# LSTM stage of a 12-sublayer decoder: the inputs' product on four column groups of 32 tokens, one copy of the turned input ahead of it, and the context loaded behind the weights

## The chip, the cores and the metric

One core of a Trainium2 chip. The metric is the device time of one execution in microseconds (us); lower is better. The kernel is one launch; its weights are repacked on the host beforehand.

## The reference, cut to what matters

The reference runs twelve sublayers on x of 8 sequences x 112 tokens x 256 features, in float32. Only the first is touched: an attention whose queries and keys come out of two LSTMs.

```python
def _lstm(x, Wih, Whh, b):
    xW = jnp.einsum('bsd,gd->sbg', x, Wih) + b          # the inputs' product
    h0 = jnp.zeros((x.shape[0], Whh.shape[1]), x.dtype)
    def step(carry, xt):
        h, c = carry
        gates = xt + h @ Whh.T                          # the recurrent product
        i, f, g, o = jnp.split(gates, 4, axis=-1)
        c = jax.nn.sigmoid(f) * c + jax.nn.sigmoid(i) * jnp.tanh(g)
        h = jax.nn.sigmoid(o) * jnp.tanh(c)
        return ((h, c), h)
    _, hs = jax.lax.scan(step, (h0, h0), xW)
...
x = x + _L0_attn_ref(_layernorm(x, axis=-1), L0_attn_Wih_q, L0_attn_Whh_q, L0_attn_b_q, ...)
```

Each LSTM has 256 hidden features (1024 gates) and 112 steps, which follow one another. A later sublayer, L0_xattn, is the first that reads the context `ctx_512` (8 x 375 x 128).

## The kernel before, in words

**Loads.** The constructor issues, on SyncE's DMA queue (SP), x, the constants (the identity among them) and a small vector, and then the first eight weight blobs into a ring of eight buffers (`_Ring.load`, L358); a further blob is issued when one has been used up, the next of them only when the LSTMs are over. The context, turned (`ctxT`, 1.5 MB), is issued on ScalarE's queue at L393, at the same time as x. The first two blobs are the q LSTM's input and recurrent weights, the next two those of the k LSTM, the fifth the biases.

**Ahead of the LSTMs (`ln_T_mm`).** The layer norm (L464 to L474, VectorE) writes `xn`. TensorE turns it in four quarters: two halves of four sequences by two halves of the features (L546, four transposes of 112x128 into a PSUM tile `mm`, of which there are two). Each quarter is copied out of PSUM twice: by VectorE into `xs`, in the order [feature half, block of 16 tokens, sequence, token] (L552), and by ScalarE into `xnT`, in the order of tokens (L556). `xs` is the stationary operand of the inputs' product; `xnT` that of the values.

**The inputs' product (`product`, L585).** One block of 16 tokens of all 8 sequences is 128 columns. `inputs(m, l, a, n)` multiplies block m with n gate columns of LSTM l, in two matmuls over the feature halves; two adds on VectorE (L610) take the result out of PSUM, add the bias and write `xw`. Block 0 of both LSTMs is computed ahead of the loop, in products of 512 columns; everything else comes from the generator `pieces`, one matmul at a time: blocks 1 to 6 in products of 256 columns, and then the values of the eight sequences (112 tokens by 256). Two pieces are taken ahead of the loop and 110 in its steps, so steps 110 and 111 have none.

**The loop (`lstm`).** Its order is written out by hand for TensorE, VectorE and ScalarE. In each step t, for LSTM l = 0 and then 1:
- L652: the recurrent product onto the gates `g`, eight matmuls, two for each of four column groups. The state `hT` is 32 columns wide, and group j writes partitions 32j to 32j+31 with a quarter of the gates.
- L615: `from_inputs` begins the gates of step t+1, four matmuls, one for each column group, which pick the step's rows out of `xw`.
- for l = 1, one piece of the inputs' product, L585 (here 128 columns wide).
- L665 and L666 (ScalarE): sigmoid and tanh of the gates; L671, L673, L674 (VectorE): the cell; for l = 1 an add of the inputs' product, L610; L678 (ScalarE): tanh of the cell; L680, L682 (VectorE): h, and its turned form `hT`, which L652 of the next step reads.
- L683 (GpSimd): a copy of `hT` into `hs`, which the attention reads after the loop.

A float32 matmul stands in the profile as two loads (PEld) and two matmuls (PE).

`cp` copies out of PSUM by VectorE and ScalarE in turn, from one flag for the whole kernel.

Of the kernel before, what the change touches and what calls it, by code (L numbers as in the profile page):

```python
# [31 lines left out]
P = 128  # L32
S, NB, D = 112, 8, 256
T = S * NB
HT = T // 2
HB = NB // 2
# [299 lines left out]
def drain(steps):  # L336

    while True:
        try:
            next(steps)  # L340
        except StopIteration as stop:
            return stop.value


class _Ring:


    def __init__(self, nc, pool, src, where, used):
        self.nc, self.pool, self.src, self.where, self.used = nc, pool, src, where, used
        self.tiles, self.dead = [], 0  # L350
        self.load()
# [22 lines left out]
class _Kernel:  # L374
    def __init__(self, ctx, tc, args, plan):
        self.tc, self.nc, self.args = tc, tc.nc, args
        nc = self.nc
        where, used, self.vw, self.cw = plan
        pool = ctx.enter_context(tc.tile_pool(name="keep", bufs=1))
        self.small = ctx.enter_context(tc.tile_pool(name="small", bufs=4))  # L380
        ring = ctx.enter_context(tc.tile_pool(name="ring", bufs=NBUF))
        self.n = 0
        self.turn = 0
        self.x = pool.tile([P, NB, D], F32, tag="x", name="x")
        nc.sync.dma_start(self.x[:S], args["in_x"].rearrange("b s d -> s b d"))
        nv, ncst = args["in_vec"].shape[1], args["in_const"].shape[1]
        self.cst = pool.tile([P, ncst], F32, tag="cst", name="cst")
        nc.sync.dma_start(self.cst, args["in_const"])
        self.vec = pool.tile([P, nv], F32, tag="vec", name="vec")
        nc.sync.dma_start(self.vec, args["in_vec"])  # L390
        self.w = _Ring(nc, ring, args["in_w"], where, used)
        self.ctxT = pool.tile([P, NB * CTX], F32, tag="ctxT", name="ctxT")
        nc.scalar.dma_start(self.ctxT, args["in_ctxT"])  # L393
        self.xn = pool.tile([P, NB, D], F32, tag="xn", name="xn")
        self.xnT = pool.tile([P, 2, T], F32, tag="xnT", name="xnT")
        self.ident = self.c("ident")
# [141 lines left out]

    def ln_T_mm(self, ps, xs):

        drain(self.normalise(self.x, self.xn))
        for half in range(2):
            for kc in range(2):
                tp = self.t(ps, [P, 512], "mm")
                for j in range(HB):
                    self.nc.tensor.transpose(  # L546
                        tp[:, j * S : (j + 1) * S],
                        self.xn[:S, half * HB + j, kc * P : (kc + 1) * P],
                        self.ident[:S, :S],
                    )  # L550
                bs = slice(half * HB, (half + 1) * HB)
                self.nc.vector.tensor_copy(  # L552
                    xs[:, kc, :, bs, :].rearrange("p m b r -> p b m r"),
                    tp[:, :HT].rearrange("p (b m r) -> p b m r", b=HB, r=16),
                )
                self.nc.scalar.copy(self.xnT[:, kc, half * HT : (half + 1) * HT], tp[:, :HT])  # L556

    def lstm(self, hs, xs, vv, ps0):

# [7 lines left out]
        nc, tc, w = self.nc, self.tc, self.w  # L569
# [5 lines left out]
        with tc.tile_pool(name="ps_lstm", bufs=2, space=PSUM) as ps, tc.tile_pool(  # L575
# [5 lines left out]

            def product(pm, lhsT, rhs, outs):

                for k in range(2):
                    nc.tensor.matmul(pm, lhsT[k], rhs[:, k, :], start=k == 0, stop=k == 1)  # L585
                    if k == 1:
                        adds.extend((out, pm[:, part], row) for out, part, row in outs)
                    yield

            def inputs(m, l, a, n):  # L590
                pm = self.t(ps0, [P, 512], "mm")[:, :n]
                steps = [xs[:, k, m, :, :].rearrange("p b r -> p (b r)") for k in range(2)]
                outs = []
                for at in range(0, n, n // 2):
                    cols = slice(a + at, a + at + n // 2)
                    outs.append((xw[:, l, m, cols], slice(at, at + n // 2), bias[l][:, cols]))
                return product(pm, steps, wih[l][:, :, a : a + n], outs)

            def values(b):
                pm = self.t(ps0, [P, 512], "mm")[:S, :D]  # L600
                out, outs = vv[:S, b].rearrange("p h d -> p (h d)"), []
                for cols in (slice(0, P), slice(P, D)):
                    outs.append((out[:, cols], cols, bv[:S, cols]))
                return product(pm, self.tokens(b), wv, outs)
# [40 lines left out]
            with tc.manual_schedule(engines={ET.PE, ET.DVE, ET.Activation}):  # L645
                for t in range(S):
                    for l in range(2):
                        g = gs[l]
                        if t > 0:
                            for c in range(2):  # L650
                                for j in G:
# [4 lines left out]
                                        start=False,  # L656
                                        stop=c == 1,
                                        skip_group_check=True,
# [1861 lines left out]
```

## Time and profile before

| | us |
|---|---|
| median of 3 runs | 2295.76 (2290.16 to 2302.23) |
| the profiled execution | 2297.48, its span 2295.6 |
| TensorE busy | 2095.2 (91%) |
| VectorE busy | 1353.8 (59%) |
| ScalarE busy | 813.3 (35%) |
| first LSTM step begins (first sigmoid, L665) | 33.48 |
| last recurrent product (L652) begins | 408.58 |

"Span" is the time from the first to the last instruction of the profiled execution. A busy TensorE is one that has matmuls in flight; their ends are modelled, so starts are the safer thing to read. In the timeline the columns are the start in us, the length of the group in us, the engine, the line and operation, output<-inputs, the array's rows*columns and the shape, the number of records, and in brackets how long the engine was idle before and what ended that. In the waits they are: who waited, for whom, the total in us, how often, and the longest.

### The profile page before, as it was taken

What the parts mean: (1) busy time and instruction counts of PE and PEld (TensorE: products, weight loads), DVE (VectorE), ACT (ScalarE), POOL (GpSimd) and SP (SyncE); (2) the same over time, 40 slices, a digit from 0 to 9 for tenths busy, and PEclk for the clock granted to TensorE, in tenths of its full rate; (3) what the DMA queues carried; (4) which work ended last, traced back from release to release, by engine and by line L of the source; (5) the groups of instructions that cost most, each with busy time, mean ns of one, the idle gap of its engine ahead of it and who ended that gap; (6) DMA issues with size and microseconds to landing.
All of it is one profiled execution on the core that took longest, in us unless ns stands there. A gap on an engine that the chain in (4) does not pass through costs nothing.

```text
span 2295.6 us, 43649 instructions
## 1 busy us (share of the span) xinstructions
PE 2095.2 (91%) x17192; PEld 1261.1 (55%) x17192; DVE 1353.8 (59%) x3894; ACT 813.3 (35%) x2336; POOL 207.5 (9%) x406
## 2 busy tenths in 40 slices
PE   6999999898998999899898988999999999799944
PEld 3444444465666566546575555566655556556623
DVE  4666666586355677643666665676710314767788
ACT  2444444461112456420232224665221011256522
POOL 0111111002012000000003422000000000100000
PEclk9999999898999999999999999999999998999956
DMA  5000001002000000011001011001200100000000
GB/s 196 3 2 2 2 21 36 31 20 101 0 1 15 19 2 20 19 34 49 1 19 38 20 64 37 2 2 38 74 37 29 44 0 1 1 1 2 2 0 16
DMA packets 9889, 57.49 MB, mean 25 GB/s; under 512 B 1114, under 2 KB 2906, under 8 KB 4698
## 3 DMA queue, kind: packets, MB, share of 16 engines
q1 hardware_dynamic: 9108, 50.01, 6.0%
q8 instruction: 137, 2.24, 0.4%
q0 software_dynamic: 432, 3.15, 0.4%
q10 hardware_dynamic: 144, 1.54, 0.2%
q14 instruction: 68, 0.56, 0.1%
HBM read 53.77 MB, written 0.92 MB: 24 GB/s over the span
## 4 chain that ended last, share of the span: by engine, by line
PE 81%; DVE 13%; ACT 3%; issue 2%; POOL 1%; DMA 0%; DVEq 0%; POOLq 0%; ACTq 0%
PE mm L428 31%; PE g L652 9%; PE gu L428 7%; PE tr L1247 6%; PE g L615 4%; PE sc L428 4%; PE mm L585 3%; PE tr L428 3%; PE av L1263 3%; PE s L428 1%; PE mm L804 1%; DVE xn L474 1%; DVE xnm L1234 1%; PE s L751 1%; PE av L428 1%
## 5 line engine op out<-in xcount | busy, mean ns | idle before, releaser
L652 PE MATMUL g<-w,hT 128*32 128x256 f32 x3552 | 236.3, 383 | 1.1 <-DVE hT L682 0.8
L1234 DVE TENSOR_REDUCE xnm<-sc 112x1 f32<-112x375 f32 x384 | 184.5, 540 | 40.8 <-PE sc L428 40.2
L1247 PEld LDWEIGHTS tr<-cst,xe 112*125 112x125 f32 x1152 | 151.4, 188 | 94.8 <-issue 37.7
L1247 PE MATMUL tr<-cst,xe 112*125 112x112 f32 x1152 | 193.0, 289 | 6.8 <-DVE xeT L1255 4.2
L428 PE MATMUL mm<-hT,w 128*128 128x448 f32 x512 | 193.0, 539 | 0.0
L652 PEld LDWEIGHTS g<-w,hT 128*32 128x32 f32 x3552 | 94.7, 109 | 107.7 <-DVE hT L682 33.1
L428 PEld LDWEIGHTS mm<-hT,w 128*128 128x128 f32 x512 | 97.1, 190 | 94.4 <-issue 94.4
L428 PE MATMUL mm<-xnT,w 128*128 128x448 f32 x316 | 134.8, 568 | 8.0 <-DVE qT L1216 2.9
L1253 ACT COPY xeT<-tr 125x336 f32<-125x336 f32 x192 | 85.4, 445 | 158.4 <-PE tr L1247 158.1
L615 PE MATMUL g<-xw,cst 128*32 128x256 f32 x1792 | 137.8, 379 | 0.0
L1255 DVE COPY xeT<-tr 125x336 f32<-125x336 f32 x192 | 97.2, 506 | 68.7 <-PE tr L1247 61.8
L428 PE MATMUL mm<-w,hT 128*112 128x256 f32 x576 | 131.2, 387 | 0.3 <-DVE x L2042 0.3
L1238 ACT ACTIVATE xe<-sc,xnm 112x375 f32<-112x375 f32 x256 | 126.6, 583 | 7.3 <-DVE xnm L1234 7.3
L428 PE MATMUL gu<-xnT,w 128*128 128x448 f32 x320 | 124.3, 543 | 1.6 <-DVE hT L1401 1.2
L428 PEld LDWEIGHTS mm<-w,hT 128*112 128x112 f32 x576 | 102.9, 181 | 26.5 <-issue 2.9
L678 ACT ACTIVATE th<-cell 128x64 f32<-128x64 f32 x224 | 57.4, 256 | 158.8 <-DVE cell L674 158.1
L2365 DVE COPY wq<-tr 128x256 bf16<-128x256 bf16 (+1 forms) x12 | 4.6, 420 | 162.7 <-PE tr L2364 162.7
L665 ACT ACTIVATE sg<-g 128x192 f32<-128x192 f32 x224 | 74.1, 331 | 73.4 <-PE g L652 63.1
L428 PEld LDWEIGHTS mm<-xnT,w 128*128 128x128 f32 x316 | 59.4, 198 | 65.7 <-issue 42.5
L428 PE MATMUL mm<-w,oT 128*112 128x256 f32 x304 | 80.3, 410 | 16.3 <-DVE oT L1875 5.3
L428 PEld LDWEIGHTS gu<-xnT,w 128*128 128x128 f32 x320 | 59.3, 190 | 61.0 <-issue 54.0
L428 PE MATMUL sc<-xkT,qT 32*112 32x375 f32 x768 | 89.8, 519 | 0.0
(451 smaller groups left out, 3647.2 us busy)
## 6 DMA issues: line engine op xcount, KB each, us to landing
w<-in_w SPq DMA_DIRECT2D x33, 1024.0 KB, 4.9
raw<-in_wq POOLq DMA_DIRECT2D x3, 1024.0 KB, 5.3
cx<-in_ctx SPq DMA_DIRECT2D x2, 1500.0 KB
w<-in_w SPq DMA_DIRECT2D x3, 896.0 KB, 4.7
wi<-in_wint SPq DMA_DIRECT2D x3, 768.0 KB, 6.0
w<-in_w SPq DMA_DIRECT2D x2, 768.0 KB, 4.1
ctxT<-in_ctxT ACTq DMA_DIRECT2D x1, 1500.0 KB, 7.9
w<-in_w SPq DMA_DIRECT2D x2, 512.0 KB, 3.5
```

Source lines behind the costliest of these rows:

```text
L428: self.nc.tensor.matmul(out, lhsT, rhs, start=i == 0, stop=i == len(pairs) - 1)
L585: nc.tensor.matmul(pm, lhsT[k], rhs[:, k, :], start=k == 0, stop=k == 1)
L615: nc.tensor.matmul(g[32 * j : 32 * j + 32, :], pick[:, t % 16, :], xw[:, l, t // 16, 256 * j : 256 * j + 256], start=True, stop=t == 0, sk ...
L652: nc.tensor.matmul(g[32 * j : 32 * j + 32, :], hT[l][:, c, :], whh[l][:, c, 256 * j : 256 * j + 256], start=False, stop=c == 1, skip_group ...
L665: nc.scalar.activation(sg[:, :192], g[:, :192], AF.Sigmoid)
L678: nc.scalar.activation(th, cell[l], AF.Tanh)
L1234: nc.vector.tensor_reduce(nm, sc, AX.X, ALU.max, negate=True)
L1238: nc.scalar.activation(e, sc, AF.Exp, bias=nm)
L1247: nc.tensor.transpose(tp[:CH, i * S : (i + 1) * S], e[:, i * CH : (i + 1) * CH], self.ident[:S, :S])
L1253: nc.scalar.copy(eT, src)
L1255: nc.vector.tensor_copy(eT, src)
L1263: nc.tensor.matmul(avs[b][32 * j : 32 * j + 32, c * S : (c + 1) * S], values[b % 2][:CH, i, 4 * c + j, :], eTs[b, c, j][:, i, :], start=i ...
```

## The change

- `product`: each matmul of 128 (or 112) columns is cut into four of 32 (for 112: three of 32 and one of 16), each writing its own 32 partitions of the PSUM tile.
- `ln_T_mm`: each turned quarter is copied out of PSUM once, into `xs`, by `cp`, so by VectorE and ScalarE in turn; GpSimd copies from `xs` to `xnT`.
- the constructor: `ctxT` is issued on SyncE's queue, behind the first eight weight blobs.

```diff
-        nc.scalar.dma_start(self.ctxT, args["in_ctxT"])
+        nc.sync.dma_start(self.ctxT, args["in_ctxT"])
...
         drain(self.normalise(self.x, self.xn))
         for half in range(2):
+            bs = slice(half * HB, (half + 1) * HB)
             for kc in range(2):
-                tp = self.t(ps, [P, 512], "mm")
-                for j in range(HB):
-                    self.nc.tensor.transpose(
-                        tp[:, j * S : (j + 1) * S],
-                        self.xn[:S, half * HB + j, kc * P : (kc + 1) * P],
-                        self.ident[:S, :S],
-                    )
-                bs = slice(half * HB, (half + 1) * HB)
-                self.nc.vector.tensor_copy(
-                    xs[:, kc, :, bs, :].rearrange("p m b r -> p b m r"),
-                    tp[:, :HT].rearrange("p (b m r) -> p b m r", b=HB, r=16),
-                )
-                self.nc.scalar.copy(self.xnT[:, kc, half * HT : (half + 1) * HT], tp[:, :HT])
+                o = xs[:, kc, :, bs, :].rearrange("p m b r -> p b m r")
+                self.cp(o, self.turned(self.xn, ps, kc, half, "mm").rearrange("p (b m r) -> p b m r", b=HB, r=16))
+                o2 = self.xnT[:, kc, half * HT : (half + 1) * HT]
+                nc.gpsimd.tensor_copy(o2.rearrange("p (b m r) -> p b m r", b=HB, r=16), o)
...
+                n = lhsT[0].shape[-1]
                 for k in range(2):
-                    nc.tensor.matmul(pm, lhsT[k], rhs[:, k, :], start=k == 0, stop=k == 1)
+                    for a in range(0, n, 32):
+                        r = slice(a, min(a + 32, n))
+                        nc.tensor.matmul(
+                            pm[r], lhsT[k][:, r], rhs[:, k, :], start=k == 0, stop=k == 1, skip_group_check=True
+                        )
```

`turned` is the helper that other stages use already: the same four transposes into a tile of the same two buffers.

More of the change, by code (lines that the diff above doesn't have):

```diff
@@ L539, in ln_T_mm @@
     def ln_T_mm(self, ps, xs):
+        nc = self.nc
         drain(self.normalise(self.x, self.xn))
         for half in range(2):
+            bs = slice(half * HB, (half + 1) * HB)
             for kc in range(2):
-                tp = self.t(ps, [P, 512], "mm")
-                for j in range(HB):
-                    self.nc.tensor.transpose(
-                        tp[:, j * S : (j + 1) * S],
-                        self.xn[:S, half * HB + j, kc * P : (kc + 1) * P],
-                        self.ident[:S, :S],
-                    )
-                bs = slice(half * HB, (half + 1) * HB)
-                self.nc.vector.tensor_copy(
-                    xs[:, kc, :, bs, :].rearrange("p m b r -> p b m r"),
-                    tp[:, :HT].rearrange("p (b m r) -> p b m r", b=HB, r=16),
-                )
-                self.nc.scalar.copy(self.xnT[:, kc, half * HT : (half + 1) * HT], tp[:, :HT])
+                o = xs[:, kc, :, bs, :].rearrange("p m b r -> p b m r")
+                self.cp(o, self.turned(self.xn, ps, kc, half, "mm").rearrange("p (b m r) -> p b m r", b=HB, r=16))
+                o2 = self.xnT[:, kc, half * HT : (half + 1) * HT]
+                nc.gpsimd.tensor_copy(o2.rearrange("p (b m r) -> p b m r", b=HB, r=16), o)
     def lstm(self, hs, xs, vv, ps0):
```

## Prediction

> **What bounds the kernel now.** I read the page's table of engines and its chain first. TensorE is busy for 91% of the span and carries 81% of the chain, so work taken off TensorE counts, if nothing else ends last in the same place. The change touches two places only: the first 33 us, and the LSTM loop from 35 to 410 us. For the loop I took the timeline of TensorE over one step in the middle and over the last two steps, then the waits of its weight loads between 34 and 408 us.
>
> ```profile
> 282.24 1.07 PE L652 MATMUL g<-w,hT 128*32 128x256 f32 x16
> 283.12 0.61 PE L615 MATMUL g<-xw,cst 128*32 128x256 f32 x8
> 283.56 1.07 PE L652 MATMUL g<-w,hT 128*32 128x256 f32 x16
> 284.45 0.61 PE L615 MATMUL g<-xw,cst 128*32 128x256 f32 x8
> 284.99 0.70 PE L585 MATMUL mm<-w,xs 128*128 128x256 f32 x2
> ...
> 403.93 1.07 PE L652 MATMUL g<-w,hT 128*32 128x256 f32 x16
> 404.81 0.61 PE L615 MATMUL g<-xw,cst 128*32 128x256 f32 x8
> 405.24 1.05 PE L652 MATMUL g<-w,hT 128*32 128x256 f32 x16
> 406.11 0.61 PE L615 MATMUL g<-xw,cst 128*32 128x256 f32 x8
> 407.12 1.07 PE L652 MATMUL g<-w,hT 128*32 128x256 f32 x16 [0.40 <-DVE hT L682]
> ```
>
> A step is: recurrent product of the first LSTM (L652), its gates from inputs (L615), the same for the second LSTM, then a piece of the inputs' product (L585). From start to start, the groups take 0.88, 0.44, 0.89, 0.54, and after L585 0.63 (the next L652 starts at 285.62): 3.38 us. Over the whole loop, L652 of step 1 starts at 35.28 and that of step 110 at 403.93: 368.65 over 109 steps, 3.38 as well. Step 110 is the one step with no L585 behind it: 407.12 less 403.93 is 3.19, and there TensorE sat idle for 0.40 and waited for hT.
>
> ```profile
> PEld mm L585 <- issue: 45.3, 110, 0.4
> PEld g L652 <- DVE hT L682: 32.3, 109, 0.9
> PEld g L652 <- DVE cell L671: 18.3, 55, 0.3
> ```
>
> Ahead of each L585 the weight loads stand still for 0.41 with no releaser ("issue"), although every other group's loads run ahead (L615's at 282.91, 0.21 before its matmuls). L585's load and matmul start together (284.99), and so do those of the L652 behind it (285.62). So going from 128x32 pieces to a 128x128 product and back empties the array both times. In the first row on L652 the second LSTM waits for its hT; the row that names cell is the first LSTM after L585, and its hT was ready at 285.37 (L682, 285.13 plus 0.24), 0.25 before: there the array was late, not hT.
>
> **The loop's product on column groups.** Two records (128 wide) become eight (32 wide), the shape of L615's x8, which frees the array after 0.44 (283.12 to 283.56) with four groups side by side. So L585 takes 0.44 where it took 0.63, and the L615 ahead of it 0.44 where it took 0.54: TensorE's own step is 0.88+0.44+0.89+0.44+0.44 = 3.09, 0.29 less. That is not the gain, because hT is late next. First LSTM: L652's start to its L682 is 2.89 (282.24 to 285.13), and from there to the next L652 0.30 (406.82 to 407.12): 3.19. Nothing in that chain changes, so no step is shorter than 3.19. Second LSTM: in the last steps it took 3.34 (405.24 to 408.58), because its L671 stands on VectorE behind the first LSTM's L682 and starts 0.57 after the start of its own sigmoid (406.42 to 406.99), against 0.37 for the first (405.12 to 405.49). That is a matter of offset: it started 1.31 behind the first and ended 1.46 behind. At 1.46 its sigmoid comes 0.15 later against the same L682, the queueing falls from 0.20 to 0.05, and its chain to 3.19. From offset 1.46 TensorE still has 0.89+0.44+0.44 to do, which is over at 3.23, against hT at 3.19; should the array be late, the offset shrinks, which frees it again. So I expect a step between 3.19 and 3.23, and take 3.21: 0.17 less over 109 steps, **18.5 us**. Bounds: 20.7 at 3.19; nothing at 3.38; a loss if the pieces do not run side by side (a rival). The eight products of the values (the last 16 pieces) have 112 tokens, so a fourth group of 16 columns: priced as one of 32. VectorE's add (L610) keeps its place, as does every instruction behind the LSTMs on each engine: four calls of the alternating copy leave its turn as it was.
>
> **A rule against this.** L615's loads at 282.91 start while L652's last matmuls stream until about 283.12, in the same rows of the array. The Trainium skill ("TensorE: Matmul & The Clock Gate", Part 3, The mechanism) says that weight loads overlap matmuls in flight only where the row group differs, and the column pieces all have the same row group. The trace disagrees; by the rule the eight loads would be exposed, which is the rival on the other side below.
>
> **Context behind the weights.** The start hangs on x:
>
> ```profile
> ctxT<-in_ctxT ACTq DMA_DIRECT2D x1, 1500.0 KB, 7.9
> x<-in_x SPq DMA_DIRECT2D x1, 896.0 KB, 10.1
> ...
> DVE st L464 <- DMA x<-in_x: 10.8, 1, 10.8
> ```
>
> Both are issued at 0.75 and share the engines, whose busy share is about 1.0 from 3 to 30 us. ctxT lands first, at 8.6; x at 10.84. Between 3 and 8.6 us some 400 GB/s moved, so 1.54 MB less ahead of x is worth **3.8 us**; x would land near 7. Bounds: 0, if x's small packets are its own limit; 5.3, if x lands like a 896 KB weight blob (4.7 after issue, 5.5). Every weight comes as much sooner: the bias of L610 (fifth blob) is 8.5 MB down the line now and 6.95 then, which the rates by window put at about 20.3, while L610 would want it near 21.3 (26.14 less 4.8). That margin of 1 us hides it. On SP's queue ctxT comes after the eight weight blobs (issued by 13.3); the next entry there is only issued at 408. ctxT's first reader is at 539.6. ScalarE loses an issue of 0.41 that nobody waited for.
>
> **One copy ahead.** Now each turned quarter is copied twice out of PSUM, by VectorE (0.62) and then ScalarE (0.53); the third quarter's transposes wait for ScalarE until 20.04, and L585 until 22.33. Then VectorE and ScalarE copy alternate quarters at once: the third transposes start at 19.45, TensorE is through the last quarter near 21.4, the first L585 follows there. **0.9 us**. A ScalarE copy with this stride isn't in the trace: 0.53 (its plain copy) to 0.62 (VectorE's same shape), which moves this by 0.1. The four copies that GpSimd gains are bounded by its 112x512 copy (0.62) and its 112x512 tensor_scalar (1.50): 2.5 to 6 us, from about 16, ahead of its hs copies, of which the first comes at about 30. The next reader of xnT is the values at 352.7. Hidden; if they were late, hs would queue and hT's writer with it, for a few steps.
>
> **The products before the loop** lose three changes of shape (27.75, 28.30, 32.79), at 0.10 to 0.19 each by the loop's rows: **0.4 us**. At the start the first L585 records take 0.85 instead of 0.43 for 3.6 us; I leave that as it is. The Trainium skill ("TensorE: Matmul & The Clock Gate", What's actually happening) has the clock released after one full window of about 3.4 us of activity, on a grid that doesn't start with the kernel; by it the half rate could last up to twice 3.4 us, and the sum would be up to 1.6 us smaller.
>
> **Sum.** 18.5+3.8+0.9+0.4 = 23.6. The profiled execution took 2297.48 (span 2295.6), 1.7 above the median 2295.76. So 2273.9 for that execution, and 2272 against the median. About 0.5% (11.5 us) is what a measurement can tell here: faster is below 2284.3.
>
> **Rivals.** (1) The recurrence keeps the step. If the second LSTM's 3.34 stays, as its last step shows, the loop gains 0.04 x 109 = 4.4, with the start 9.5: 2286, no change. For it: that row. Against it: the offset, which grows in that very step. 11%. (2) Slower: the loads of the column pieces are exposed, as the rule above has it. Eight loads of 0.109 are 0.87, the step 3.09+0.87 = 3.96, 0.58 more over 109 steps, 63; the 80 loads before the loop 8.7, less the start's 5.1: 67 slower, 2362. It decides from some 0.3 exposed per step. For it: L585's loads stand still now. Against it: the 48 loads of L615 and L652 in each step have the same shape and are covered wherever hT is there in time. 8%. (3) x lands no earlier: 3.8 less, 2276. Inside the forecast's range.
>
> **How the numbers follow.** Forecast with (3) 80%, a slip between it and (1) 1%. Low end: step at 3.19 and x at 5.5 give 3.7 more, and the runs shown reach 5.6 below their median: 2263. High end: rival (1) with a little spread, 2287. Outside is rival (2) and the tail of (1). Faster 0.80, same 0.12, slower 0.08.
>
> **What would show it.** Right: L652 of the first LSTM every 3.2 us; no "issue" idle ahead of L585's loads; L652 waiting for hT in both LSTMs, offset near 1.45; L585 x8 in 0.6; x landing near 7; first L585 before 18. Wrong: a step over 3.3, loads of L585 that start with their matmuls, L585 to next L652 over 0.5, or the clock at 0.5 inside the loop (1.00 in every window now), which would double TensorE's 3.09 of a step.

## The result, and the profile after

The changed kernel takes 2266.43 us, the median of 3 runs (2266.06 to 2273.7), against 2295.76. The ratio is 0.9885, 95% interval 0.986 to 0.9909: some 26 us, of which the interval allows 21 to 32. Its profiled execution took 2266.43, span 2264.7, so 30.9 less of span than the one of before. Predicted were 23.6.

The timeline of a middle step, with the same columns as before (L651 is the recurrent product, L614 the gates from inputs, L582 the inputs' product):

```profile
272.78 1.06 PE L651 MATMUL g<-w,hT 128*32 128x256 f32 x16
...
273.65 0.61 PE L614 MATMUL g<-xw,cst 128*32 128x256 f32 x8
...
274.22 1.07 PE L651 MATMUL g<-w,hT 128*32 128x256 f32 x16
...
275.11 0.61 PE L614 MATMUL g<-xw,cst 128*32 128x256 f32 x8
...
275.54 0.61 PE L582 MATMUL mm<-w,xs 128*32 128x256 f32 x8
...
275.99 1.07 PE L651 MATMUL g<-w,hT 128*32 128x256 f32 x16
```

From the first LSTM's recurrent product to its next one it is 3.21 us (272.78 to 275.99), where it was 3.38. The product has eight records and gives the array back after 0.45, where it took 0.63; L614 ahead of it takes 0.43, where that took 0.54. The second LSTM now starts 1.44 behind the first, where it started 1.32 behind.

The waits of the weight loads inside the loop had five rows before (34 to 408 us), with 45.3 us of "issue" at their head. Three stand in the prediction. The larger of the other two is the first LSTM again, right behind the product, put down to another instruction of VectorE that had just ended; the first row below is that one, of before. After (28 to 386 us) a single row is left, the second below:

```profile
PEld g L652 <- DVE tmp L673: 16.7, 50, 0.3
```

```profile
PEld g L651 <- DVE hT L681: 82.9, 218, 0.9
```

Nothing stands still ahead of the product any more, and of the 222 recurrent products in steps 1 to 111, of both LSTMs, 218 wait for hT. The bound has passed from the array to the recurrence. In the same stretch of steps the product's loads run while the matmuls of L614 stream:

```profile
271.91 0.61 PE L614 MATMUL g<-xw,cst 128*32 128x256 f32 x8
272.13 0.35 PEld L582 LDWEIGHTS mm<-w,xs 128*32 128x32 f32 x8
...
272.35 0.61 PE L582 MATMUL mm<-w,xs 128*32 128x256 f32 x8
```

The start, by the DMA issues and by the waits of the first 36 us:

```profile
x<-in_x SPq DMA_DIRECT2D x1, 896.0 KB, 5.8
```

```profile
DVE st L464 <- DMA x<-in_x: 6.5, 1, 6.5
DVE xw L609 <- DMA w<-in_w: 3.7, 1, 3.7
```

x lands 5.8 us after its issue instead of 10.1, and the layer norm begins at 6.53 instead of 10.84. The second row is new: the first add of the inputs' product (20.54) is put down to the biases' transfer. First matmul of the inputs' product: 16.89 (22.33 before). First sigmoid: 26.71 (33.48 before).

Three stretches of the two profiles, cut at the first sigmoid (L665 before, L664 after) and at the start of the last transposed hT, with the time behind the loop in which TensorE ran at half clock (the clock events of the trace grant it either the full clock or half of it):

| us | before | after | less |
|---|---|---|---|
| up to the first sigmoid | 33.48 | 26.71 | 6.8 |
| loop | 378.05 | 360.56 | 17.5 |
| behind the loop | 1884.1 | 1877.4 | 6.7 |
| of that at half clock | 221.9 | 193.7 | 28.2 |

The first two make 24.3, against the 23.6 of the prediction. The third had no term in it. So two questions were left for experiments: whether the array was emptied by the change of shape, with the recurrence ending last now, and whether the 6.7 behind the loop belong to the change.

### The profile page after: what moved, and what is told of

Read it like the earlier page. It is cut to its first block, busy times and chain, and to the rows that moved or that the text cites. A ratio compares the mean times of both kernels' runs of the same rounds, so it can differ in the third digit from the quotient of the medians.

```text
span 2264.7 us, 45090 instructions
## 1 busy us (share of the span) xinstructions
PE 2065.6 (91%) x17912; PEld 1249.3 (55%) x17912; DVE 1351.4 (60%) x3892; ACT 814.7 (36%) x2334; POOL 210.1 (9%) x410
## 3 DMA queue, kind: packets, MB, share of 16 engines
q0 software_dynamic: 432, 3.15, 0.4%
## 4 chain that ended last, share of the span: by engine, by line
PE 79%; DVE 14%; ACT 3%; issue 2%; POOL 1%; DMA 0%; DVEq 0%; POOLq 0%; ACTq 0%
PE mm L428 31%; PE g L651 9%; PE gu L428 7%; PE tr L1246 6%; PE g L614 4%; PE sc L428 4%; PE tr L428 3%; PE av L1262 3%; PE mm L582 2%; PE mm L803 1%; PE s L428 1%; DVE xnm L1233 1%; DVE xn L474 1%; PE av L428 1%; PE s L750 1%
## 5 line engine op out<-in xcount | busy, mean ns | idle before, releaser
L651 PE MATMUL g<-w,hT 128*32 128x256 f32 x3552 | 236.7, 384 | 1.8 <-DVE hT L681 1.5
L651 PEld LDWEIGHTS g<-w,hT 128*32 128x32 f32 x3552 | 93.2, 109 | 121.8 <-DVE hT L681 82.9
L614 PE MATMUL g<-xw,cst 128*32 128x256 f32 x1792 | 137.9, 379 | 0.0
L664 ACT ACTIVATE sg<-g 128x192 f32<-128x192 f32 x224 | 74.2, 331 | 66.9 <-PE g L651 45.6
```

What stands on the lines that cost most here:

```text
L614: nc.tensor.matmul(g[32 * j : 32 * j + 32, :], pick[:, t % 16, :], xw[:, l, t // 16, 256 * j : 256 * j + 256], start=True, stop=t == 0, sk ...
L651: nc.tensor.matmul(g[32 * j : 32 * j + 32, :], hT[l][:, c, :], whh[l][:, c, 256 * j : 256 * j + 256], start=False, stop=c == 1, skip_group ...
L664: nc.scalar.activation(sg[:, :192], g[:, :192], AF.Sigmoid)
```

## The experiments

**The three parts alone.** Each is one hunk of the change put into the kernel before: `product`, the issue of `ctxT`, or `ln_T_mm`. The changed kernel was run again on the same chip, and a third time later on another.

> The kernel before with the inputs' product on four column groups, nothing else. Theory (the changes of shape emptied the array, now the recurrence sets the step): a step of 3.20 to 3.22 where it was 3.38, the loop from first sigmoid to last transpose 360.5 where it was 378.0, no idle 'issue' ahead of the product's loads; first sigmoid near 32.7 (33.5 less about 0.8 for the shapes ahead of the loop); 18 to 19 us faster, ratio 0.992. Rival (the gain needs the earlier start as well, or what lies behind the loop got faster by the product): the part behind the loop is shorter than before by some 6 us at the same time at half clock, ratio 0.989.

> The kernel before with the context issued on SyncE's queue behind the weights, nothing else. Theory: x lands at 6.5 where it landed at 10.8, the first sigmoid 4.3 earlier (29.2), the loop as before (378), about 4 us faster, ratio 0.998. Rival (the part behind the loop gained 6.6 us because the transfers now stand otherwise): 9 to 11 us faster, ratio 0.995 to 0.996, with the part behind the loop shorter at the same time at half clock.

> The kernel before with one copy out of PSUM per quarter and GpSimd's copies, nothing else. Theory: x at 10.8 as before, first matmul of the inputs' product 1.1 earlier (near 21.2), first sigmoid 32.4, loop 378, 1 us faster, not to be told from no change in the time. Rival (GpSimd's copies in the way of hs or of VectorE): first sigmoid or loop later than before.

> The changed kernel once more. Theory (start 6.8, loop 17.5, and the rest is the clock gate behind the loop, which falls otherwise in each execution): first sigmoid 26 to 27.5, loop 360.5, the part behind the loop anywhere from 1875 to 1885 as its time at half clock is 195 to 225; about 24 us faster on the mean of rounds, ratio 0.9895. Rival (the change shortens the part behind the loop): that part at 1877 again and the ratio at or below 0.988.

| | ratio to before (95%) | x lands | first sigmoid | loop | behind | at half clock |
|---|---|---|---|---|---|---|
| product_only | 0.9915 (0.9895 to 0.9936) | 11.2 | 32.09 | 360.4 | 1884.5 | 221.9 |
| context_only | 0.9977 (0.9964 to 0.999) | 7.4 | 30.14 | 378.4 | 1873.4 | 194.6 |
| copy_only | 0.9979 (0.9964 to 0.9994) | 11.7 | 32.66 | 378.2 | 1880.7 | 201.8 |
| after_again | 0.9881 (0.9858 to 0.9904) | 6.7 | 27.41 | 360.6 | 1881.3 | 210.8 |

One of the twelve executions of copy_only took 5843.69 us; nothing on record says why, and its ratio is worked out without it.

The whole gain of the loop is in the product alone (360.4), with x as late as ever. The context moves x by 3.4 in this execution and nothing else in the start or the loop. The copy takes the stretch from x to the first product from 11.49 (22.33 less 10.84) to 10.36 (22.02 less 11.66), with the loop as before, so GpSimd's copies are in nobody's way. In the time of whole runs context and copy each show some 5 us, of which the copy's profile accounts for 1; their intervals reach down to 2.3 and 1.4 us.

Behind the loop, the rival that the change had made that part faster fails: the changed kernel itself needed 1881.3 there this time, and the kernel with nothing but the context moved 1873.4, less than any other. What goes with it is the time at half clock. Over all 13 profiles of this case the part behind the loop lies between 1873.4 and 1887.4 and the half-clock time in it between 193.7 and 222.9, with a correlation of 0.91 and a slope of 0.34 us per us. That is a correlation; no run sets the clock.

> The changed kernel again, to be compared on one chip with the two others: first sigmoid 26.5 to 27.5, loop 360.5, part behind the loop 1877 to 1885 as its time at half clock goes; ratio 0.988.

0.9903 (0.9884 to 0.9922); first sigmoid 26.80, loop 360.4, behind it 1882.4 with 216.1 at half clock. So three profiles of one kernel differ by 5.0 behind the loop and by 0.2 in it.

**Is it the change of shape?** The changed kernel with two groups of 64:

```diff
-                    for a in range(0, n, 32):
-                        r = slice(a, min(a + 32, n))
+                    for a in range(0, n, 64):
+                        r = slice(a, min(a + 64, n))
```

> The changed kernel with the inputs' product cut into two groups of 64 columns instead of four of 32; all else as changed. Theory (a change of the array's shape empties it, whichever way): loads of the product stand still for some 0.4 us in each step again and start with their matmuls, the step 3.36 to 3.38, the loop 377 to 379, about 17.5 slower than the changed kernel. Rival (only a full 128-column load cannot run ahead): no idle ahead of the loads, the step 3.20, the loop 360.5.

The timeline of TensorE's loads and matmuls, and the waits of the loads from 60 to 360 us, in that kernel:

```profile
270.34 0.20 PEld L582 LDWEIGHTS mm<-w,xs 128*64 128x64 f32 x4 [0.41 <-issue]
270.34 0.65 PE L582 MATMUL mm<-w,xs 128*64 128x256 f32 x4
```

```profile
PEld mm L582 <- issue: 36.6, 89, 0.4
```

The idle 0.41 is back, load and matmul start together, and the step is 3.31 here (the next L582 at 273.65), the loop 375.5; ratio 0.995 (0.9931 to 0.9968). So loads of 64 columns don't run ahead either, between groups of another shape. The loop is 15.0 longer than with 32, where 17.5 were expected. Four records of 64 leave the array 0.05 sooner than two of 128 (0.58 from L582 to L651, 0.63 before), but only every second step is that much shorter: 3.31 and 3.39 in turn, 3.36 and 3.39 before.

One rival is left: that any load wider than 32 columns has to wait, whatever stands ahead of it. The old kernel's own start answers it. There twelve matmuls of 128 columns follow one another, ahead of the loop:

```profile
28.30 4.56 PE L585 MATMUL mm<-w,xs 128*128 128x512 f32 x12
```

```profile
28.30 0.30 PEld L585 LDWEIGHTS mm<-w,xs 128*128 128x128 f32 x2 [0.41 <-PE mm L585]
28.83 0.19 PEld L585 LDWEIGHTS mm<-w,xs 128*128 128x128 f32 x1 [0.24 <-issue]
29.26 0.19 PEld L585 LDWEIGHTS mm<-w,xs 128*128 128x128 f32 x1 [0.24 <-issue]
```

The first two loads are over at 28.60, and the second matmul starts only at 28.83; each further load runs while the matmul before its own streams. So loads of 128 columns do run ahead where the neighbour has their shape, and it is the change of shape that holds them back.

**How far is the array behind the recurrence?** Two experiments: each matmul of the product issued twice (`for a in [*range(0, n, 32)] * 2`), and the loop's pieces left out, with `xw` beyond block 0 and the values set to zero by GpSimd.

> The changed kernel with each matmul of the inputs' product issued twice (the second pass adds into the result again, so xw is not the reference's). Theory (in the changed kernel TensorE's 3.09 to 3.10 and the recurrence's 3.19 stand close together): TensorE ends last again, the step 3.52 to 3.54, the loop near 395. Rival (TensorE has real room under the recurrence): the step below 3.4. Rival (column pieces do not run side by side): more than 3.6.

> The changed kernel without any piece of the inputs' product in the loop (left out: xw of the blocks 1 to 6 and the values, which are set to zero by GpSimd ahead of the loop, and their adds). Theory (the recurrence sets the step now): a middle step of 3.18 to 3.20, so the product in its new form costs at most 0.02 a step. Rival (the array still ends last): the step falls to 3.1 or less.

The timeline of TensorE with the product twice:

```profile
270.25 0.61 PE L614 MATMUL g<-xw,cst 128*32 128x256 f32 x8
270.68 1.05 PE L582 MATMUL mm<-w,xs 128*32 128x256 f32 x16
271.55 1.05 PE L651 MATMUL g<-w,hT 128*32 128x256 f32 x16
272.41 0.61 PE L614 MATMUL g<-xw,cst 128*32 128x256 f32 x8
272.84 1.05 PE L651 MATMUL g<-w,hT 128*32 128x256 f32 x16
273.70 0.61 PE L614 MATMUL g<-xw,cst 128*32 128x256 f32 x8
```

From L614 to L614 it is 3.45 (270.25 to 273.70): 0.43, 0.87, 0.86, 0.43, 0.86, no gap. The mean step of the loop is 3.47. The expected 3.52 to 3.54 was too high: a recurrent product gives the array back after 0.86 where its loads ran ahead, and after 0.87 to 0.89 where load and matmul start together, as in the rows that I had added up. Take one piece of 0.43 off, and TensorE's own step in the changed kernel is 3.02 by this estimate, not 3.09. Its idle time lies ahead of the second LSTM (in the step shown first, the array is free 0.43 after 273.65, and L651 starts at 274.22); behind the product, array and hT come within some 0.02 us of each other.

Without any piece in the loop the regular step is 3.22, with the two LSTMs 1.5 to 1.7 apart (L648 there, at 270.00, 271.63 and 273.22), the loop 362.7. I had expected 3.18 to 3.20; the array as the bound would have given 3.1 or less. With the pieces the regular steps are 3.19 and 3.22 in turn, so in its new form the product costs the loop nothing.

The 0.03 between 3.19 and 3.22 lies in one place. VectorE starts the transposition that makes hT 0.33 us behind the start of h in some steps and 0.36 in others: in the old and the changed kernel 0.36 in the odd steps of the first LSTM and 0.33 otherwise, in no_pieces 0.36 in every step of both. Step 110, which gave the 3.19, is an even one. What makes the 0.03 the traces don't show.

**A shorter chain.** If the recurrence ends last, the time between gates and hT should count. The sigmoid of o is only needed for h, so it can come behind the tanh of g; and the piece of the product can stand between the two LSTMs (`if l == 0`).

```diff
-                        nc.scalar.activation(sg[:, :192], g[:, :192], AF.Sigmoid)
+                        nc.scalar.activation(sg[:, :128], g[:, :128], AF.Sigmoid)
                         nc.scalar.activation(sg[:, 192:], g[:, 192:], AF.Tanh)
+                        nc.scalar.activation(sg[:, 128:192], g[:, 128:192], AF.Sigmoid)
```

> The changed kernel with the gates' sigmoid cut in two: i and f (128 columns) first, then the tanh of g, then the sigmoid of o, which only h needs. Theory (the recurrence sets the step, so what shortens its chain shortens the step until TensorE's 3.10): tanh starts 0.05 to 0.07 earlier after the gates, the step 3.13 to 3.16, the loop 353 to 356, 5 to 7 us faster than the changed kernel, ratio 0.985 to 0.986 to the kernel before. Rival (the array is as close a bound, or ScalarE's third operation gets in the way): the step stays at 3.20 or grows.

> The split gates, and the piece of the inputs' product issued behind the first LSTM's gates instead of the second's. Theory (with the sigmoid cut, step and array meet again where the piece stands ahead of the first LSTM's recurrent product; between the two LSTMs there is room for it): step 3.13 to 3.16, loop 351 to 354, 6 to 8 us faster than the changed kernel on the same chip. Rival (the two LSTMs then meet on VectorE, as in the run without pieces, whose step was 3.22): step 3.18 to 3.22, no faster than the changed kernel.

> The changed kernel with the piece issued behind the first LSTM's gates, the gates uncut. Theory (the recurrence alone sets the step): 3.19 to 3.22, loop 359 to 362, as the changed kernel. Rival (in the changed kernel the array still costs something where the piece stands): step below 3.19.

The regular steps in the table are those of the first LSTM, from hT to hT (L681).

| | ratio to before (95%) | regular steps | loop |
|---|---|---|---|
| the changed kernel (first profile) | 0.9885 (0.986 to 0.9909) | 3.19 and 3.22 in turn | 360.6 |
| split_gates | 0.9878 (0.9856 to 0.9899) | 3.15 and 3.21 in turn | 357.9 |
| balanced | 0.9893 (0.9875 to 0.9911) | 3.15 and 3.24 in turn | 359.7 |
| piece_early | 0.9907 (0.9889 to 0.9926) | 3.20 and 3.24 in turn | 361.9 |

Cutting the sigmoid brings 2.7 us of the loop and not 5 to 7: in its timeline L582 at 271.03 is followed by L651 at 271.46, the 0.43 of a full array, while the second LSTM waits for hT. Moving the piece gives that back. None of them can be told from the changed kernel by its time. Why balanced gains no more, with the product out of the way, is not settled.

## Why the prediction was right

**The loop.** Its mechanism held in each point: no idle "issue", both LSTMs waiting for hT, an offset of 1.44 (1.46 forecast), regular steps of 3.19 and 3.22 (3.21 forecast). That 3.21 met the mean is luck in part: it was taken as the middle between the chain's 3.19 and an array done at 3.23, and what the traces show is the chain itself, at 3.19 and 3.22 in turn.

It brought 17.5 of the 18.5, as some steps in each profile are about 0.28 longer. In the three profiles of the changed kernel these are the same six steps, and each goes back to one instruction of VectorE or ScalarE that starts 0.2 to 0.3 us later than in other steps. The transposition in step 90 is one, 0.69 behind its h instead of 0.33:

```profile
317.18 0.23 DVE L679 TENSOR_TENSOR h<-sg,th 128x64 f32<-128x64 f32 x1 [0.38 <-ACT th L677]
317.87 0.24 DVE L681 STREAM_TRANSPOSE hT<-h 128x64 f32<-128x64 f32 x1 [0.46 <-DVE h L679]
```

Here the trace names no other engine as what it waited for, so the cause stays open. Step 110 of the old profile, the only one without a piece behind it, gave both the bound and the way the offset would move. The term that was mis-sized is TensorE's own step, 3.02 for 3.09; it did not decide.

**Context and copy.** x came 4.3 sooner for the 3.8 by bytes, inside the bounds of 0 and 5.3. SyncE's queue is not empty until 408, as the prediction and the text on the kernel before have it: weight blobs are issued at 323.10, 350.08 and 353.85 too (302.03 is the first after the change). The context, issued at 10.73 and landed at 31.76, is in front of them all the same. The copies brought 1.1 for 0.9: 11.49 from x to the first product before, 10.36 after. The margin of 1 us that was to hide the biases was none: the transfer is named as the last to come in the changed kernel and in copy_only, where nothing of the weights was moved. The biases landed at 20.43, close to the 20.3 forecast (24.77 before); it is the need that came sooner than the 21.3 forecast. In after_again the array is named, with the add at 20.78, so the wait is at most some tenths, and the stretch behind it is no longer for it (5.06 us from the first L614 to the first sigmoid, and 5.05 in after_again).

**The products ahead of the loop.** 0.4 was too small. The stretch from the first L615 (L614 after) to the first sigmoid is 5.73 in before and context_only and 5.74 in copy_only, and 5.06, 5.06 and 5.05 in after, product_only and after_again: 0.67. One of the three changes of shape, the one at 27.75, lies in front of that stretch. From the first product to the first L615 it is 5.42, 5.52 and 4.90 in the three kernels with the old product and 4.76, 4.36 and 5.29 in the three with the new one. TensorE begins this stretch at half clock, for 3.63, 3.85 and 2.59 us and for 2.66, 1.86 and 3.72. With half of that time taken off, 3.60 are left with the old product and 3.43 with the new: 0.17 more, 0.84 in all. The other 0.49 that this stage gained in the first profile (11.15 to 9.82 from the first product to the first sigmoid) is the shorter time at half clock, 2.66 for 3.63, and no part of the change. So the start's 6.8 are 4.3 of x, 1.1 of the copies, 0.8 of the shapes and 0.5 of the clock.

**What no term held.** 6.7 us behind the loop. The two later profiles of the same kernel keep 2.8 and 1.7 of them, and they have more time at half clock; so the first result was lucky in how the clock fell there. The range had 5.6 for the spread of the runs, which is what kept the median inside it.

**The rivals.** That the recurrence would keep the step at 3.34 failed with the offset: the second LSTM's chain is 3.19 and 3.22 now. That the loads of column pieces would be exposed failed: L582's loads at 272.13 run under L614's matmuls, and even 16 in a row (piece_twice) leave no gap. By the rule of the Trainium skill ("TensorE: Matmul & The Clock Gate", Part 3, The mechanism) loads of one row group would not overlap; the trace disagrees, 0.21 ahead in each step. By the Trainium skill ("TensorE: Matmul & The Clock Gate", What's actually happening) the prediction allowed up to twice 3.4 us of half rate at the start. In 13 profiles the trace's clock event came 1.5 to 3.9 us after the first product's matmul, and in 8 of them sooner than 3.4, so that sentence's loss of up to 1.6 was never seen.

## What to carry to other kernels

A loop whose matmuls mostly use one shape of the array pays for each one of another shape: here 0.29 us for a 0.43 us product, going in and coming out, and the sign of it is a weight load that starts together with its own matmul behind an idle with no releaser (an idle alone is none: the loads at 28.83 and 29.26 have one too, and are ahead of their matmuls). Cut that matmul into the others' shape; eight records then cost no more array time than two. Before adding up what that frees, find a step in the old profile where the work is missing: it shows what ends last next, and so how much of the gain remains.

## What the runs showed of the hardware

- Loads of 64 columns between groups of 32 stand still as those of 128 do (0.41 in each). Loads of 128 columns between matmuls of 128 run ahead: twelve such matmuls took 4.56 us, with each load under the matmul before.
- Identical code behind the loop takes 1873 to 1887 us in 13 profiles, on average 0.34 us more for each us at half clock (correlation 0.91). A difference of 6.7 us in one pair of profiles says nothing on the change, unless the stage where it arises has been looked at.
- A transfer of 896 KB in 1 KB packets landed 5.8 us after issue when it went first on its queue, and 10.1 when 1.5 MB from another queue shared the engines; over the 13 profiles it is 5.4 to 6.6 in the ten of the first kind and 10.1 to 10.9 in the three of the second.
